# Moving weight combinations from VectorE to GpSimd in the first steps of a two-layer FFN kernel

## The chip, the cores and the metric

The kernel runs on one core of one Trainium2 chip. The metric is the device time of that core in microseconds (us), from one launch. Engines go by the profile's names: PE (TensorE), PEld (its weight loads), DVE (VectorE), ACT (ScalarE), POOL (GpSimd), SP (SyncE, which issues most of the loads). ACTq, SPq and POOLq are the engines' instruction queues.

## The reference

Only the first layer's feed-forward product matters here. With x of 32 x 128 x 2048, seen as 4096 rows of 2048:

```python
out = jnp.einsum('bsd,od->bso', x, W) + bias
xa  = jnp.einsum('bsd,erd->ebsr', x, A)
upd = jnp.einsum('ebsr,eor,e->bso', xa, Bf, coeffs * scales)
return out + upd
```

The x that enters it is first mixed by a kernel per batch row (eight mixed 128 x 128 matrices). Around the product there are a residual, a grouped convolution of nine taps, and a second feed-forward of 16 heads over permuted channels. All values are float32.

## The kernel before, in words

**One weight for both terms.** The low-rank update is folded into the weight: W' = W^T + A^T (w Bf), with w = coeffs * scales. W' is made in 16 blocks of 128 x 2048, `blocks`, named (kh, oh, kc): half of the contraction, half of the output, and one of four row tiles. `a_load` (L126) loads half h of A and then scales it by w on DVE (L135); `b_load` loads Bf. `w_load` (L154, on SP) loads a block of W^T. `w_make` (L160) makes one of the first four blocks by eight matmuls (L170), each pair added to the tile by DVE (L174), and stores the block with `w_store` (L158, a 1 MB DMA issued by POOL into `wb_d`). `w_make_two` (L203) makes two blocks at a time for the other twelve, in seven products (PE L208, DVE L211).

**Two levels of Strassen-Winograd.** The big product takes seven outer rounds, `ROUNDS` = P1, P2, P6, P7, P5, P3, P4, each over eight groups g of 512 rows of x: 56 steps. Step 0 is (P1, g = 0), step 8 is (P2, g = 0). Each step is one `multiply` (L318): seven inner products in the order P1, P2, P6, P5, P7, P3, P4, each over four row tiles kc, into the PSUM banks px, py, pz (PE L334). ACT copies a product to the result tile m_P where it is the first there (L329), DVE adds the others (L327). px goes on being accumulated in the later products, so PE waits until what stood there was read. `between(j)`, called after each inner product, hangs other work in: w loads for the next step (j = 2), row sums of W' (`row_sums`, L228, and L955/L956), all on DVE.

**Combinations.** An inner product needs sums of quarters. `x_combine` (L275) makes four for x on POOL (s_P, L285 to L288). For the weights a tile t has quarters b11, b12, b21, b22, and `inner_weights` (L230) makes t1 = b12 - b11, t2 = b22 - t1, b12 = b22 - b12 in place, t4 = b21 - t2: tiles P_t and the quarter b12 itself. Product P5 uses t1, P6 uses t2, P7 the new b12, P4 uses t4. In round P1 the first three are made on DVE (L873 to L875) piece by piece behind each `w_make`, and b12 on DVE in step 0 after `w_make_two` (L917), each behind an addition of the old b12 to the row sum (L916). `x_outer` (L298) makes two sums of three x tiles on POOL, in place, for later rounds (L302, L304), each stored by POOL (s_d, L262). `a_combine` makes sa (POOL), `b_combine` makes tb.

**What sets the order.** It is written out by hand: each engine runs its instructions in program order. All large tiles share 24 slots of 1 MB (`slot`), so a new tile waits for the last use of an older one, stores included. For step i the loop does, in order: x loads and `x_combine` of step i + 1, `x_outer`, `inner_weights` of the next round (only in rounds P2 and later, in the last step of the round), in round P1 `w_make_two` for two more blocks, `multiply`. In round P1 the combinations for P2 come behind the last `multiply` of the round.

Of the kernel before, what the change touches and what calls it, by code (L numbers as in the profile page):

```python
# [11 lines left out]
ALU = mybir.AluOpType  # L12
# [4 lines left out]
P = 128  # L17
B = 32
L = 2048
QW = 512  # L20
# [12 lines left out]
NG = B // GB  # L33
# [14 lines left out]
ROUNDS = ("P1", "P2", "P6", "P7", "P5", "P3", "P4")  # L48
# [3 lines left out]
def adaln_ffn_kernel(  # L52
# [16 lines left out]
    nc = tc.nc  # L69
# [8 lines left out]
    def slot(name, shape=(P, L)):  # L78
        return big.tile(list(shape), FP, name=name, tag="s")
# [46 lines left out]
    def a_load(h, k0, k1):  # L126
        for ki in range(2):
            i0 = (2 * h + ki) * QW
            nc.sync.dma_start(
                a_sb[h][:, :, ki, k0:k1].rearrange("p c k i -> p c (k i)"),  # L130
                A[:, :, i0 + k0 * P : i0 + k1 * P],
            )
        for c in range(2):
            cols = a_sb[h][:, c, :, k0:k1]
            nc.vector.tensor_scalar(cols, cols, wsc[:, c : c + 1], None, ALU.mult)  # L135

    def b_load(h, q, o0=0, n=QW):
        i0 = (2 * h + q) * QW + o0
        nc.sync.dma_start(bf_sb[h][:, :, q, o0 : o0 + n], BfT[:, :, i0 : i0 + n])
# [12 lines left out]
    def w_load(kh, oh, kc):  # L152
        t = slot(f"w_{kh}{oh}{kc}", (P, 2, 2, QW))
        nc.sync.dma_start(t.rearrange("p k o c -> p (k o c)"), WT[kh, oh, kc])  # L154
        return t
# [4 lines left out]
    def w_make(k, t):  # L160

        kh, oh, kc = k
        for oi in range(2):
            for ki in range(2):
                pw = bank()

                n = QW // 2 if k == (0, 0, 0) and oi == 0 else QW
                for o0 in range(0, QW, n):
                    for c in range(2):
                        nc.tensor.matmul(  # L170
                            pw[:, o0 : o0 + n], lhsT=a_sb[kh][:, c, ki, kc],
                            rhs=bf_sb[oh][:, c, oi, o0 : o0 + n], start=(c == 0), stop=(c == 1),
                        )
                nc.vector.tensor_tensor(t[:, ki, oi], pw, t[:, ki, oi], ALU.add)  # L174
                done(pw)
        w_store(k, t)
# [50 lines left out]
        for ki in range(2):  # L227
            nc.vector.tensor_tensor(wsum[:, oh], wsum[:, oh], t[:, ki], ALU.add)  # L228

    def inner_weights(name, ts):  # L230

        t1, t2, t4 = (slot(f"{name}_t{k}", (P, 4, QW)) for k in (1, 2, 4))
        tt = nc.gpsimd.tensor_tensor
        for kc, t in enumerate(ts):
            b11, b12, b21, b22 = (t[:, ki, oi] for ki in range(2) for oi in range(2))
            tt(t1[:, kc], b12, b11, ALU.subtract)
            tt(t2[:, kc], b22, t1[:, kc], ALU.subtract)  # L237
            tt(b12, b22, b12, ALU.subtract)
            tt(t4[:, kc], b21, t2[:, kc], ALU.subtract)
        return weights(ts, t1, t2, t4)  # L240

    def weights(ts, t1, t2, t4):
        return {
            "P1": [t[:, 0, 0] for t in ts], "P2": [t[:, 1, 0] for t in ts],
            "P3": [t[:, 1, 1] for t in ts], "P7": [t[:, 0, 1] for t in ts],
            "P4": [t4[:, kc] for kc in range(4)], "P5": [t1[:, kc] for kc in range(4)],
            "P6": [t2[:, kc] for kc in range(4)],
        }
# [596 lines left out]
    nc.sync.dma_start(cs, coeffs)  # L845
    nc.vector.tensor_tensor(wsc, cs[:, 0:2], cs[:, 2:4], ALU.mult)
    a_load(0, 0, 1)
    b_load(0, 0, 0, QW // 2)
    b_load(0, 0, QW // 2, QW // 2)
    b_load(0, 1)  # L850
    a_load(0, 1, 4)
    wt = {k: w_load(*k) for k in blocks[0:2]}
    xs = {0: [x_load(0, 0, 0)]}
    for k in blocks[2:4]:
# [7 lines left out]
    lhs, sa, tb = {}, {}, {}  # L862
    sa[0] = a_combine(0, nc.gpsimd.tensor_tensor)
    first = [wt.pop(k) for k in blocks[0:4]]
    t1, t2, t4 = (slot(f"P1_t{k}", (P, 4, QW)) for k in (1, 2, 4))
    for kc, t in enumerate(first):
        k = blocks[kc]
        w_make(k, t)
        made.append(k)
        if kc == 1:  # L870
            lhs[0] = x_combine(*steps[0], xs.pop(0))
        tt = nc.vector.tensor_tensor
        tt(t1[:, kc], t[:, 0, 1], t[:, 0, 0], ALU.subtract)  # L873
        tt(t2[:, kc], t[:, 1, 1], t1[:, kc], ALU.subtract)
        tt(t4[:, kc], t[:, 1, 0], t2[:, kc], ALU.subtract)  # L875
    rhs = weights(first, t1, t2, t4)
    tb[1] = b_combine(1, nc.vector.tensor_tensor)
    a_load(1, 0, 4)
    unsummed, unsummed_first = [], list(first)
# [9 lines left out]
    for i, (r, g) in enumerate(steps):  # L889
        ri = i // NG  # L890
        last_round = ri + 1 == len(ROUNDS)
        if i + 1 < len(steps):
            if i + 1 not in xs:
                xs[i + 1] = x_loads(*steps[i + 1])
            if not last_round:
                lhs[i + 1] = x_combine(*steps[i + 1], xs.pop(i + 1))
                x_outer()
        if i + 2 < len(steps) and ri > 0 and not last_round:
            xs[i + 2] = x_loads(*steps[i + 2])
        if i == 0:  # L900
            olds_load(0)
        if i + 1 < len(steps) and not last_round:
            olds_load(i + 1)
        if g == NG - 1 and 0 < ri < len(ROUNDS) - 1:
            nxt = inner_weights(ROUNDS[ri + 1], [nxt[kc] for kc in range(4)])

        if ri == 0:
            ks = blocks[4 + 2 * g : 6 + 2 * g]
            if ks:
                two = [wt.pop(k) for k in ks]  # L910
                w_make_two(ks, two, sa[ks[0][0]], tb[ks[0][1]])
                made.extend(ks)
                if g == 0:
                    for kc, t in enumerate(first):
                        b12 = t[:, 0, 1]
                        nc.vector.tensor_tensor(wsum[:, 0, 1], wsum[:, 0, 1], b12, ALU.add)  # L916
                        nc.vector.tensor_tensor(b12, t[:, 1, 1], b12, ALU.subtract)  # L917
                if g == 1:
                    sa[1] = a_combine(1, nc.gpsimd.tensor_tensor)
                if g == 3:  # L920
                    tb[0] = b_combine(0, nc.gpsimd.tensor_tensor)
                for k, t in zip(ks, two):
                    unsummed.append((k[1], t))
                    if k[:2] == (1, 0):
                        nxt[k[2]] = t
        elif ri + 1 < len(ROUNDS):
            for k, combine in waiting.items():
                nxt[k] = combine()
            waiting = {}
            if 2 <= g < 6:  # L930
                waiting[g - 2] = outer_weights(ROUNDS[ri + 1], g - 2)

        if last_round and g == 0:
            late_loads()
        if last_round and g == 2:

            late["te"] = mix.rearrange("p (k r) c -> p k r c", k=2)
            nc.sync.dma_start(mix.rearrange("p k c -> p (k c)"), te_d)
        k0 = 3 * (g - NG)
        if last_round:  # L940
            stage(k0, stage_first)

        def between(j):
            b = (ri - 1) * (NG - 2) + g
            if ri > 0 and g < NG - 2 and b < B and j < KEXP // 2:
                mixed_kernel(b, (2 * j, 2 * j + 1))
            if ri == 0 and j == 2:
                for k in blocks[6 + 2 * g : 8 + 2 * g]:
                    wt[k] = w_load(*k)
            if ri == 0 and j in (1, 3) and unsummed:  # L950
                row_sums(*unsummed.pop())
            if ri == 0 and j == 5 and unsummed_first:
                t = unsummed_first.pop(0)
                tt = nc.vector.tensor_tensor
                tt(wsum[:, 0, 0], wsum[:, 0, 0], t[:, 0, 0], ALU.add)  # L955
                tt(wsum[:, 0], wsum[:, 0], t[:, 1], ALU.add)  # L956
            if last_round:
                if j == 3 and i + 1 < len(steps):
                    lhs[i + 1] = x_combine(*steps[i + 1], xs.pop(i + 1))
                    olds_load(i + 1)  # L960
                if j in (2, 4):
                    stage(k0 + j // 2, stage_first)
                if j % 2:
                    stage_third(k0 + j // 2)
                else:
                    stage(k0 + j // 2, stage_second)

        multiply(r, g, lhs.pop(i), rhs, olds.pop(i), between)
        next(chain, None)
        if last_round and g >= 6:  # L970
            pair(g - 6)
        if last_round and g == 7:
            rings()
            gather_two(0)
        if g == NG - 1 and ri + 1 < len(ROUNDS):
            if ri == 0:
                nxt = inner_weights(ROUNDS[ri + 1], [nxt[kc] for kc in range(4)])
            rhs = nxt
            nxt = {}

# [83 lines left out]
```

## Time and profile before

| | us |
|---|---|
| median of three runs | 2672.01 (2669.6 to 2672.71) |
| profiled execution | 2672.8 |
| its span, first to last instruction | 2671.0 |
| PE busy | 2624.4 |
| DVE busy | 1404.4 |
| POOL busy | 1117.0 |
| ACT busy | 535.2 |

The span is what the profile pages and all times on its axis refer to; 1.8 us lie around it. A line of a timeline gives the start, the duration, the engine, the line of the kernel, what is written from what, how many instructions are merged, and in brackets how long the engine was idle before and what ended that. A line of waits reads: who waited for whom, total, times, longest. A line of windows gives the stretch, its length, the busy time of each engine with its instruction count, the clock granted to PE (1.00 is full), the mean share of the DMA engines and GB/s.

### The profile page before, as it was taken

To read this page: it belongs to the slowest core of one execution; us is meant where nothing else is said; L and a number is where in the kernel's file an instruction comes from. 1 tells how busy PE (TensorE), PEld (TensorE's weight loads), DVE (VectorE), ACT (ScalarE), POOL (GpSimd) and SP (SyncE) were. 2 spreads that over 40 slices of the span, in tenths; PEclk is the share of its full clock that TensorE was granted. 3 is DMA by queue.
4 is the path that set the end of the run, shared out by engine and by line. 5 is a ranking of instruction groups with operands and counts; after the bars stand their busy time and mean duration, and the time that the engine had idled before them with its cause. 6 is when DMAs were issued, how large, how long until landed. Compare 5 with 4: busy or idle time off the path is not lost.

```text
span 2671.0 us, 19893 instructions
## 1 busy us (share of the span) xinstructions
PE 2624.4 (98%) x6484; PEld 1233.8 (46%) x6484; DVE 1404.4 (53%) x2188; ACT 535.2 (20%) x1103; POOL 1117.0 (42%) x750
## 2 busy tenths in 40 slices
PE   7999999999999999999998999999999999999998
PEld 3444444444444444444444554544555544555543
DVE  5766145233344355454266666666666666666610
ACT  0100100000000000000001144444444444444432
POOL 4554455624736521755333333434333343333222
PEclk8999999999999999999999999999999999999999
DMA  8776548445456366555576788777787777877532
GB/s 330 298 298 265 210 182 327 184 154 209 188 228 256 145 267 267 218 211 232 201 250 183 253 298 272 225 231 234 242 253 225 229 227 233 250 235 235 164 127 87
DMA packets 183607, 609.16 MB, mean 228 GB/s; under 512 B 16848, under 2 KB 88016, under 8 KB 139088
## 3 DMA queue, kind: packets, MB, share of 16 engines
q1 hardware_dynamic: 148928, 466.40, 49.7%
q0 software_dynamic: 34144, 140.53, 15.3%
q10 hardware_dynamic: 432, 0.96, 0.1%
q8 instruction: 52, 0.85, 0.1%
q14 instruction: 51, 0.42, 0.0%
HBM read 364.03 MB, written 210.24 MB: 215 GB/s over the span
## 4 chain that ended last, share of the span: by engine, by line
PE 90%; DVE 5%; DMA 2%; POOL 1%; issue 1%; SPq 0%; ACT 0%; POOLq 0%; DVEq 0%
PE bank L334 46%; PE bank L679 16%; PE bank L690 16%; PE bank L537 6%; PE bank L447 4%; PE bank L208 2%; DVE ags L409 2%; DMA a_sb<-in_A 1%; DMA w<-in_WT 1%; DVE u L327 0%; DMA xt<-in_xT 0%; DVE vb L519 0%; DVE wsum L916 0%; DMA ws<-in_ffw 0%; DVE vb L516 0%
## 5 line engine op out<-in xcount | busy, mean ns | idle before, releaser
L679 PE MATMUL bank<-t,ws 128*128 128x512 f32 x1024 | 460.4, 592 | 0.4 <-DMA ws<-in_ffw 0.4
L690 PE MATMUL bank<-gl,ws 128*128 128x512 f32 x1024 | 460.2, 592 | 0.0
L682 ACT ACTIVATE gl<-bank 128x512 f32<-128x512 f32 x512 | 306.1, 598 | 446.4 <-PE bank L679 444.1
L334 PE MATMUL bank<-P_t,s_P 128*128 128x512 f32 x896 | 393.9, 592 | 1.5 <-POOL P_t L237 1.5
L327 DVE TENSOR_TENSOR u<-bank,u 128x512 f32<-128x512 f32 x280 | 187.3, 687 | 387.4 <-PE bank L334 378.3
L697 POOL DMA_INDIRECT out<-t,orow x128 | 152.8, 1194 | 567.5 <-DVE t L695 501.2
L690 PEld LDWEIGHTS bank<-gl,ws 128*128 128x128 f32 x1024 | 194.9, 190 | 232.7 <-issue 230.3
L679 PEld LDWEIGHTS bank<-t,ws 128*128 128x128 f32 x1024 | 194.7, 190 | 227.0 <-issue 219.1
L334 PE MATMUL bank<-wo_P,s_P 128*128 128x512 f32 x640 | 285.4, 596 | 5.5 <-DVE u L327 5.5
L334 PEld LDWEIGHTS bank<-P_t,s_P 128*128 128x128 f32 x896 | 170.4, 190 | 215.0 <-issue 211.9
L438 ACT ACTIVATE bank<-w,aggb 128x512 f32<-128x512 f32 x128 | 80.8, 684 | 894.5 <-DMA w<-w_d 876.4
L695 DVE TENSOR_TENSOR t<-bank,t 128x512 f32<-128x512 f32 x128 | 87.9, 687 | 315.5 <-PE bank L690 315.5
L430 POOL TENSOR_TENSOR x<-x,fb 128x1024 f32<-128x1024 f32 x64 | 155.3, 2446 | 220.8 <-DMA x<-in_x 192.0
L327 DVE TENSOR_TENSOR p<-bank,p 128x512 f32<-128x512 f32 x112 | 77.4, 691 | 246.7 <-PE bank L334 244.9
L334 PEld LDWEIGHTS bank<-wo_P,s_P 128*128 128x128 f32 x640 | 121.6, 191 | 161.3 <-issue 148.5
L409 DVE SCALAR_TENSOR_TENSOR ags<-mix,att_bc,ags 128x128 f32<-128x128 f32 x224 | 182.9, 816 | 4.5
L334 PE MATMUL bank<-wo_P,xt 128*128 128x512 f32 x384 | 169.0, 592 | 0.0
L663 POOL DMA_INDIRECT t<-hx_d,row x128 | 125.0, 977 | 56.4 <-issue 25.5
L285 POOL TENSOR_TENSOR s_P<-xt 128x512 f32<-128x512 f32 x40 | 52.0, 1300 | 227.3 <-DMA xt<-in_xT 200.7
L334 PE MATMUL bank<-P_t,xt 128*128 128x512 f32 x320 | 144.1, 593 | 2.6 <-DVE m_P L327 1.6
L537 PE MATMUL bank<-va,tw_l 128*128 128x256 f32 x512 | 122.4, 380 | 8.9 <-DVE va L520 7.6
L537 PEld LDWEIGHTS bank<-va,tw_l 128*128 128x128 f32 x512 | 96.8, 190 | 51.3 <-issue 36.4
(159 smaller groups left out, 2864.5 us busy)
## 6 DMA issues: line engine op xcount, KB each, us to landing
xt<-in_xT SPq DMA_DIRECT2D x64, 1024.0 KB, 8.8
u<-u_d SPq DMA_DIRECT2D x40, 1024.0 KB, 10.6
wo_P<-wb_d SPq DMA_DIRECT2D x36, 1024.0 KB, 12.5
u<-c_d SPq DMA_DIRECT2D x64, 512.0 KB, 6.0
x<-in_x SPq DMA_DIRECT2D x32, 1024.0 KB, 7.8
xg<-x SPq DMA_DIRECT2D x256, 128.0 KB, 5.9
hx_d<-x1t SPq DMA_DIRECT2D x32, 1024.0 KB, 5.4
hx_d<-ht SPq DMA_DIRECT2D x32, 1024.0 KB, 7.2
```

The source lines that it names most:

```text
L327: nc.vector.tensor_tensor(to, ps, to, ALU.add)
L334: nc.tensor.matmul(ps, lhsT=lhs[k][:, bass.ts(kc, P)], rhs=rhs[k][kc], start=first and kc == 0, stop=last and kc == 3, skip_group_check=True,)
L409: nc.vector.scalar_tensor_tensor(ag, mix[:, k], att, ag, ALU.mult, ALU.add)
L430: nc.gpsimd.tensor_tensor(xt[:, f : f + 2], xt[:, f : f + 2], late["fb"][:, f : f + 2], ALU.add)
L447: nc.tensor.matmul(pm, lhsT=ag, rhs=u[:, f], start=False, stop=True, skip_group_check=True)
L537: nc.tensor.matmul(out, lhsT=w[:, 2 * i + r], rhs=rhs, start=first and r == 0, stop=last and r == 1, skip_group_check=True,)
L663: nc.gpsimd.indirect_dma_start(out=t.rearrange("p k t -> p (k t)"), out_offset=None, in_=hx_d[g].rearrange("l k t -> l (k t)"), in_offset= ...
L679: nc.tensor.matmul(pu, lhsT=w[:, m * P : (m + 1) * P], rhs=t[:, 0], start=True, stop=True)
L682: nc.scalar.activation(gl[m], pu, AF.Gelu)
L690: nc.tensor.matmul(pd, lhsT=w[:, (MC + m) * P : (MC + m + 1) * P], rhs=gl[m], start=(m == 0), stop=(m == MC - 1),)
L695: nc.vector.tensor_tensor(t[:, 1], pd, t[:, 1], ALU.add)
L697: nc.gpsimd.indirect_dma_start(out=out, out_offset=bass.IndirectOffsetOnAxis(ap=orow[:, g, h : h + 1], axis=0), in_=t[:, 1], in_offset=None,)
```

## The change

The scale is split from `a_load` as `a_scale`; for the second half of A it is called in step 1, behind `w_make_two`, instead of ahead of step 0. `inner_weights` gets a hook, `between`, and round P1 uses it too: all four combinations of the first four blocks, and the addition of the old b12 to the row sum, are now on POOL, each block's right behind its `w_make`; `x_combine` of step 0 stands ahead of the third block's. The combinations for round P2 are issued in the step before the last of round P1, ahead of its `w_make_two` place and `multiply`, instead of behind the last `multiply`.

```diff
-        for c in range(2):
+    def a_scale(h, k0, k1):
+        for c in range(2):
             cols = a_sb[h][:, c, :, k0:k1]
             nc.vector.tensor_scalar(cols, cols, wsc[:, c : c + 1], None, ALU.mult)
...
-    def inner_weights(name, ts):
+    def inner_weights(name, ts, between=lambda kc: None):
...
         for kc, t in enumerate(ts):
+            between(kc)
...
-    t1, t2, t4 = (slot(f"P1_t{k}", (P, 4, QW)) for k in (1, 2, 4))
-    for kc, t in enumerate(first):
-        k = blocks[kc]
-        w_make(k, t)
-        made.append(k)
-        if kc == 1:
+
+    def make_first(kc):
+        t = first[kc]
+        w_make(blocks[kc], t)
+        made.append(blocks[kc])
+        if kc == 2:
             lhs[0] = x_combine(*steps[0], xs.pop(0))
-        tt = nc.vector.tensor_tensor
-        tt(t1[:, kc], t[:, 0, 1], t[:, 0, 0], ALU.subtract)
-        tt(t2[:, kc], t[:, 1, 1], t1[:, kc], ALU.subtract)
-        tt(t4[:, kc], t[:, 1, 0], t2[:, kc], ALU.subtract)
-    rhs = weights(first, t1, t2, t4)
+        nc.gpsimd.tensor_tensor(wsum[:, 0, 1], wsum[:, 0, 1], t[:, 0, 1], ALU.add)
+
+    rhs = inner_weights("P1", first, make_first)
...
-        if g == NG - 1 and 0 < ri < len(ROUNDS) - 1:
+        if g == NG - (1 if ri else 2) and ri < len(ROUNDS) - 1:
             nxt = inner_weights(ROUNDS[ri + 1], [nxt[kc] for kc in range(4)])
...
-                if g == 0:
-                    for kc, t in enumerate(first):
-                        b12 = t[:, 0, 1]
-                        nc.vector.tensor_tensor(wsum[:, 0, 1], wsum[:, 0, 1], b12, ALU.add)
-                        nc.vector.tensor_tensor(b12, t[:, 1, 1], b12, ALU.subtract)
                 if g == 1:
+                    a_scale(1, 0, 4)
                     sa[1] = a_combine(1, nc.gpsimd.tensor_tensor)
...
-            if ri == 0:
-                nxt = inner_weights(ROUNDS[ri + 1], [nxt[kc] for kc in range(4)])
```

More of the change, by code (lines that the diff above doesn't have):

```diff
@@ L239, in inner_weights @@
             tt(t4[:, kc], b21, t2[:, kc], ALU.subtract)
-        return weights(ts, t1, t2, t4)
-    def weights(ts, t1, t2, t4):
         return {
@@ L847, in adaln_ffn_kernel @@
     a_load(0, 0, 1)
+    a_scale(0, 0, 1)
     b_load(0, 0, 0, QW // 2)
@@ L851, in adaln_ffn_kernel @@
     a_load(0, 1, 4)
+    a_scale(0, 1, 4)
     wt = {k: w_load(*k) for k in blocks[0:2]}
```

## The prediction

> **What bounds the kernel now.** I read the page first: TensorE (PE) is busy nearly all the span, so only its gaps can be won.
>
> ```profile
> PE 2624.4 (98%) x6484; PEld 1233.8 (46%) x6484; DVE 1404.4 (53%) x2188; ACT 535.2 (20%) x1103; POOL 1117.0 (42%) x750
> ```
>
> Next, what PE waited for in the first 350 us, where all edits lie (total, times, longest):
>
> ```profile
> PE bank L208 <- DVE w L211: 13.6, 3, 12.8
> PE bank L334 <- DVE w L917: 1.7, 3, 1.3
> PE bank L334 <- DVE m_P L327: 1.6, 1, 1.6
> PE bank L334 <- POOL P_t L237: 1.5, 1, 1.5
> ```
>
> These are the edits' targets: 12.8 us once, 3.3 us in step 0's multiply, 1.5 us at the change of round. Then the windows of those stretches (busy PE, PEld, DVE, ACT, POOL; granted clock; DMA share):
>
> ```profile
> 36.00:52.00 16.00, 3.17 (x9) 1.18 (x7) 7.11 (x12) 0.00 (x0) 0.54 (x1) 0.74 1.02 420
> 52.00:64.00 12.00, 12.00 (x22) 5.23 (x23) 8.30 (x13) 0.00 (x0) 11.31 (x7) 0.78 0.40 165
> 64.00:92.00 28.00, 24.73 (x56) 10.13 (x55) 26.24 (x18) 3.18 (x5) 15.20 (x9) 1.00 0.75 287
> ```
>
> PE stands still to 51.9 and restarts at a reduced clock: 20 matmul records take 11.4 us there, 8.6 at the later pace (56 in 24.03). DMA is saturated to 52. Timeline of DVE:
>
> ```profile
> 49.75 1.42 DVE L135 TENSOR_SCALAR a_sb<-a_sb,wsc 128x1024 f32<-128x1024 f32 x2 [8.79 <-DMA a_sb<-in_A]
> 51.09 2.48 DVE L211 TENSOR_TENSOR w<-bank,w 128x512 f32<-128x512 f32 x4
> 67.82 5.36 DVE L917 TENSOR_TENSOR w<-w 128x512 f32<-128x512 f32 x1
> 73.10 5.47 DVE L916 TENSOR_TENSOR wsum<-wsum,w 128x512 f32<-128x512 f32 x1
> ```
>
> The evictions stood behind a scale that waited for its load. Timelines of POOL and ACT, and the load queue's waits:
>
> ```profile
> 52.29 1.26 POOL L285 TENSOR_TENSOR s_P<-xt 128x512 f32<-128x512 f32 x1 [15.07 <-DMA xt<-in_xT]
> 57.30 4.53 POOL L302 TENSOR_TENSOR xt<-xt,xt 128x2048 f32<-128x2048 f32 x1
> 62.13 0.56 POOL L262 DMA_DIRECT2D s_d<-xt  x1 [0.30 <-POOL xt L302]
> 62.71 4.52 POOL L304 TENSOR_TENSOR xt<-xt,xt 128x2048 f32<-128x2048 f32 x1
> ```
> ```profile
> 66.96 1.28 ACT L329 ACT_TABLE_LOAD   x1 [66.96 <-PE bank L334]
> 68.25 0.58 ACT L329 COPY m_P<-bank 128x512 f32<-128x512 f32 x1
> ```
> ```profile
> SPq L154 <- DMA s_d<-xt: 51.7, 3, 32.1
> ```
>
> This is the hidden second chain. The first s_d store lands at 62.1 + 4.5 = 66.6, and ACT's semaphore instructions for L329 run at 66.6: m_P of step 0 reuses the slot of an x tile that L302/L304 and this store must release. PE's first product ends at about 66.9, so now the tie costs nothing. The w loads of step 1 wait for the next two s_d stores (issued 71.7 and 79.3, landing in 5.0 and 10.8 us). A late POOL can thus stop PE twice; the instruction order of the changed kernel, with the semaphore each instruction waits on, keeps all three ties. Last, landings of the wb_d stores (minimum/median/maximum, first 110 us):
>
> ```profile
> DMA to landing us min/median/max: 8.4/9.2/11.9
> ```
>
> **The Trainium skill.** "DMA: Bandwidth & Descriptors", section "Anatomy of one DMA — SWDGE (gpsimd) path", prices a GpSimd DMA at 2.0 us plus bytes at 436 GB/s: estimate 4.4 us for 1 MB. The trace agrees on free engines (4.1 and 4.5 for the first s_d stores), not under the load stream: 8.4, 8.7, 9.4, 9.1 for the first four wb_d. "SBUF — State Buffer", section "SBUF: two separate sides", says a DVE operation with two SBUF inputs and a GpSimd one lock each other out; agreed, 5.4 us against 0.69 above. "TensorE: Matmul & The Clock Gate", section "What's actually happening", gives half clock after an idle window of about 3.4 us; the 0.74 and 0.78 agree.
>
> **The change, part by part.**
>
> *Scale a step later.* Two DVE instructions (1.42 us) move behind step 1's evictions (w_make_two); the load's place on SP is unchanged. sa[1], after them on POOL, is first needed in step 2: at nothing; that step's work covers 1.4 us. The last L174 ends at 36.4, the four b_combine take 2.6, so L211 runs at 39.0 and PE resumes at 39.8, not 51.9. Both w tiles land by 39.6. At full clock (10 pairs of 0.86) step 0's multiply starts at **48.4**, not 63.3.
>
> *DVE to POOL.* DVE loses 12 combinations and 8 sum/b12 instructions. PE sets the pace of w_make (DVE already waits for it at its end), so this gains nothing before 36. POOL gains 20 of 1.26 us (16 P_t rows of the round change run 321.06 to 341.23). New is a wait: b12 overwrites what the wb_d store of its tile reads, and in the changed order it waits for that store's landing. Behind it on POOL stand t4, the next piece's store and combinations, and x_combine of steps 0 and 1, then x_outer (L302/L304) with its stores:
> - sa ends 18.7 (last one 1.3, unstretched). Store 0 then, landing 18.7 + 8.4 = 27.0; b12, t4 to 29.6.
> - Store 1 lands 29.6 + 9.4 = 39.0; to 41.6.
> - Store 2 lands 41.6 + 9.1 = 50.7, behind x_combine (5.0) and three combinations: no wait; to 53.5.
> - Store 3: 53.5 + 4.5 = 58.0, as on free engines (the last x load landed at 57.1 with four stores ahead of it; with three, a megabyte or 2.4 us sooner); to 60.55.
> - Step 1's x_combine ends 60.55 + 5.0 = 65.6, when L302 starts: **8.3 us later** than 57.3.
>
> These combinations themselves are in time: the last t2 is made at 57.8, PE could use it at 57.9. But the first s_d store lands at 65.6 + 9.3 = 74.9; table load 1.28, copy 0.58: PE's third product, which adds to the bank that ACT must first copy, starts at about **76.9**; without the tie it would be 55.3. It has idled 21 us, so half clock: before lost 2.8 in such a restart; bounds 1.7 to 3.4 (half of one to two windows of 3.4), I take 2.55. Five products of 3.43 are 17.2: multiply ends 76.9 + 17.2 + 2.55 = **96.6**, against 91.7. So the 12.8 us and the 3.3 us are both spent: **+4.9**. Row sums stuck behind L302/L304 now fall beside products with slack; that cover gone costs up to 1.5.
>
> Step 1's second w load, landing at 90.0 before, lands at 98.3; PE reaches its need at about 100.2: slack 2. Bounds 0 and +3. Behind that load on SP stand the p_d store and step 2's x loads, which need multiply's end anyway. The late wb_d stores (6, 12, 17 us) are read only rounds later: at nothing.
>
> *P2's combinations one step sooner.* 16 POOL instructions (20.2 us) pass x_combine of step 8, and on SP nothing is reordered. On the clock of before they run from 304.4, where the last x_outer store is issued, to 324.6 (now 341.2); x_combine of step 8 ends at 329.6 (now 321.1), its second row at 327.1, PE's use of it is at 334.6. The 1.5 us wait goes: **-1.5** (bounds 0, -2).
>
> Between 104 and 325 PE idles 1 us in 221, and loads follow PE, so nothing absorbs the shift. The sum is +4.9 - 1.5 = **+3.4**. The profiled execution took 2672.8 (span 2671.0), 0.8 above the median: 2676.2 there, **2675.5** on the median's scale. About 0.2% (5.3 us) is what a measurement of this kernel can tell from no change.
>
> **The rivals.**
> 1. *Slower: the stores land later still.* Price: each us on the chain of stores 0, 1 and 3 is a us of PE. Later wb_d stores took 11.9 at worst; 11 us for the first two and 6.5 for store 3 add 2.6 + 1.6 + 2 = 6.2: +9.6. It decides from +1.9 on. For it: the loads saturate DMA (share 1.02). Against it: the first four lie within 8.4 to 9.4. The step 1 load landing over 2 us late ends there too.
> 2. *Faster: the chain is short.* If stores landed in 4.5 us, the x load (52.2) would again start step 1's x_combine: L302 at 57.3, third product at 68.6, multiply ends 88.3, so -3.4 - 1.5 = -4.9; with that load 2.4 us earlier (1 MB less store traffic before it), -7.3. Against it: those stores run beside saturated loads.
> 3. *Slot tie not binding.* If m_P did not wait, multiply would end at 72.4, but the w load at 98.3 would hold the second block: about +5.9 - 1.5 = +4.4. Same answer by another wait.
>
> **How the numbers follow.** Late chain as sized, with its bounds (+0.5 to +7): 0.68, of which about a quarter lies over +5.3. Rival 3: 0.10, half over. Rival 1: 0.12. Rival 2: 0.10, of which 0.07 beyond -5.3. So faster 0.07, same 0.59, slower 0.34. Range 2670.5 to 2681.5: -1.5 to +9.5, leaving out the rest of rival 2 and the worst of rival 1.
>
> **What would show it.** Right: PE runs w_make_two without a gap over 2 us by 40; b12 (L241 of the changed kernel) on POOL waiting for wb_d twice, 4 and 5 us; L302 first at about 65.6; PE's gap moved into step 0's multiply, some 20 us, released by ACT L329; no P_t wait near 340. Wrong: L302 before 60, no gap after 55, or a second gap, in step 1's w_make_two.

## The result, and the profile after

The changed kernel takes 2676.2 us (median of 22 runs, 2672.47 to 2679.8), the kernel before 2672.8 (22 runs, 2669.6 to 2675.89): ratio 1.0013, 95% interval 1.0006 to 1.0019, or +3.5 us (+1.6 to +5.1). The forecast was +3.4. The profiled execution took 2674.35, span 2672.6.

```profile
PE 2623.7 (98%) x6484; PEld 1234.4 (46%) x6484; DVE 1385.7 (52%) x2168; ACT 535.1 (20%) x1103; POOL 1142.4 (43%) x770
```

DVE is 19 us less busy and POOL 25 us more, as 20 instructions moved; PE's own work is the same. Lines have moved: w_make_two is L210 with its evictions L213, b12 is L241, the row sums are L230. What PE waited for in the first 350 us, from the table of waits after:

```profile
PE bank L334 <- ACT m_P L329: 22.3, 1, 22.3
PE bank L210 <- DVE w L213: 1.3, 3, 0.6
```

The four waits that the edits aimed at are gone, but for rests of at most 0.6 us, and one new one of 22.3 us stands in their place. PE's timeline shows where:

```profile
39.92 5.39 PE L210 MATMUL bank<-tb,sa 128*128 128x512 f32 x12 [0.57 <-DVE w L213]
48.58 7.03 PE L334 MATMUL bank<-w,xt 128*128 128x512 f32 x16
77.87 8.96 PE L334 MATMUL bank<-P_t,s_P 128*128 128x512 f32 x16 [22.26 <-ACT m_P L329]
96.96 3.60 PE L210 MATMUL bank<-bf_sb,a_sb 128*128 128x512 f32 x8
```

Sixteen matmuls in a line are two products. PE starts step 0's multiply at 48.58 instead of 63.29, does two products, and stands before the third. Step 1's w_make_two starts at 96.96 instead of 91.66: the 14.7 us won are lost, and 5.3 more. POOL's and ACT's timelines give the chain behind that wait:

```profile
27.69 1.27 POOL L241 TENSOR_TENSOR w<-w 128x512 f32<-128x512 f32 x1 [4.11 <-DMA wb_d<-w]
39.60 1.27 POOL L241 TENSOR_TENSOR w<-w 128x512 f32<-128x512 f32 x1 [5.03 <-DMA wb_d<-w]
52.59 1.26 POOL L241 TENSOR_TENSOR w<-w 128x512 f32<-128x512 f32 x1 [1.07 <-DMA wb_d<-w]
66.84 4.49 POOL L302 TENSOR_TENSOR xt<-xt,xt 128x2048 f32<-128x2048 f32 x1
71.62 0.57 POOL L262 DMA_DIRECT2D s_d<-xt  x1 [0.30 <-POOL xt L302]
```
```profile
75.94 1.28 ACT L329 ACT_TABLE_LOAD   x1 [75.94 <-DMA s_d<-xt]
```

b12 waits for the landing of the block's own store, three times, 10.2 us in all. So x_outer starts at 66.84 instead of 57.30, its first store lands at 75.9, and only then may ACT write m_P. At the change of round the third and fourth products of step 8 now run as one piece:

```profile
339.95 7.03 PE L334 MATMUL bank<-P_t,s_P 128*128 128x512 f32 x16
```

Before, the third was split by 1.5 us of waiting. The fifth starts at 346.82 instead of 343.26: +3.6. The two profiled spans differ by 1.6 only; after 350 us PE's waits sum to 12.6 us in this execution and 15.9 in the one of before, in stages that the change doesn't touch, and the medians, which differ by 3.4, do not carry that difference.

### The profile page after: what moved, and what is told of

The parts are those of the page before. It is cut to its first block, busy times and chain, and to the rows that moved or that the text cites. A ratio compares the mean times of both kernels' runs of the same rounds, so it can differ in the third digit from the quotient of the medians.

```text
span 2672.6 us, 19881 instructions
## 1 busy us (share of the span) xinstructions
PE 2623.7 (98%) x6484; PEld 1234.4 (46%) x6484; DVE 1385.7 (52%) x2168; ACT 535.1 (20%) x1103; POOL 1142.4 (43%) x770
## 4 chain that ended last, share of the span: by engine, by line
PE 92%; DVE 4%; POOL 2%; issue 1%; DMA 1%; SPq 0%; ACT 0%; POOLq 0%; DVEq 0%; ACTq 0%
PE bank L334 47%; PE bank L679 16%; PE bank L690 16%; PE bank L537 6%; PE bank L447 4%; PE bank L210 2%; DVE ags L409 2%; DVE u L327 0%; DVE vb L516 0%; DMA ws<-in_ffw 0%; DVE vb L519 0%; DVE va L517 0%; DMA a_sb<-in_A 0%; DVE va L518 0%; POOL wsum L874 0%
## 5 line engine op out<-in xcount | busy, mean ns | idle before, releaser
L334 PE MATMUL bank<-P_t,s_P 128*128 128x512 f32 x896 | 395.6, 595 | 22.3 <-ACT m_P L329 22.3
L663 POOL DMA_INDIRECT t<-hx_d,row x128 | 125.4, 980 | 54.6 <-issue 25.2
## 6 DMA issues: line engine op xcount, KB each, us to landing
wo_P<-wb_d SPq DMA_DIRECT2D x36, 1024.0 KB, 12.6
```

What stands on the lines that cost most here:

```text
L334: nc.tensor.matmul(ps, lhsT=lhs[k][:, bass.ts(kc, P)], rhs=rhs[k][kc], start=first and kc == 0, stop=last and kc == 3, skip_group_check=True,)
L663: nc.gpsimd.indirect_dma_start(out=t.rearrange("p k t -> p (k t)"), out_offset=None, in_=hx_d[g].rearrange("l k t -> l (k t)"), in_offset= ...
```

## The experiments

Two theories went in. **Chain**: a gain of PE before its third product of step 0 is worth nothing, since that product waits for POOL's x_outer, its store and ACT; POOL's lateness is the price, and the waits on landing stores make it. **Additive**: each edit is worth what the wait it removes shows.

All ratios are to the kernel before, run beside each kernel (medians 2673.5 and 2673.7 us).

**1. The later scale alone** (scale_only).

```diff
-        for c in range(2):
+    def a_scale(h, k0, k1):
+        for c in range(2):
...
                 if g == 1:
+                    a_scale(1, 0, 4)
```

> The kernel before with only the scale of A's second half moved to step 1. Chain theory (in step 0 PE can go no further than product P2 until GpSimd has finished the first x_outer sum, its store has landed and ACT has copied the first product): PE starts step 0's multiply at 48.4 instead of 63.3, then stands until about 68.6, restarts at half clock, and step 1's w_make_two starts at about 88.0 instead of 91.7: -3.7 us. Additive theory (each edit is worth what the wait it removes shows): 12.1 us of stall and 2.8 us of half clock go, -14.9 us.

Ratio 0.9990 (0.9982 to 0.9999): -2.7 us, between -4.8 and -0.3. POOL's and PE's timelines:

```profile
54.30 1.73 POOL L287 TENSOR_TENSOR s_P<-xt 128x512 f32<-128x512 f32 x1 [17.41 <-DMA xt<-in_xT]
60.55 4.49 POOL L304 TENSOR_TENSOR xt<-xt,xt 128x2048 f32<-128x2048 f32 x1
```
```profile
50.03 7.03 PE L336 MATMUL bank<-w,xt 128*128 128x512 f32 x16
71.58 10.10 PE L336 MATMUL bank<-P_t,s_P 128*128 128x512 f32 x16 [14.52 <-ACT m_P L331]
```

Removing a wait of 12.8 us bought a wait of 14.5 us. That excludes the additive -14.9. The expected 68.6 came at 71.58: the x load landed at 54.2 instead of 52.2 in this execution, and x_combine took 6.3 us instead of 5.0 beside DVE operations with two inputs from SBUF. In the trace step 1's w_make_two starts at 91.82, 0.2 later than before, so the -2.7 of the times is not seen in this stretch; it lies at the edge of what is resolved, and its cause is not shown. One candidate lies in later stages, behind two short gaps of PE near 1405 and 1465 us that both traces have: eight matmuls there take 3.60 and 3.67 us in this trace and 5.29 and 5.30 in the one of before, at a granted clock of 0.5 for some 3 us each time. That is 3.4 us. The mean granted clock of the runs points the same way (0.9952 in 13 runs, 0.9944 in 35 of before).

**2. P2's combinations alone** (p2_only): only the condition on g, and no call behind the round.

```diff
-        if g == NG - 1 and 0 < ri < len(ROUNDS) - 1:
+        if g == NG - (1 if ri else 2) and ri < len(ROUNDS) - 1:
```

> The kernel before with only the combinations for round P2 issued one step sooner. Both theories: the 1.5 us wait of PE at 337.4 goes and nothing else moves: -1.5 us, step 1's w_make_two stays at 91.7, step 8's third product follows its second without a gap.

Ratio 0.9989 (0.9981 to 0.9997): -2.9 us, between -5.1 and -0.8, which holds the -1.5. PE's timeline has the two products in one piece:

```profile
334.38 7.03 PE L334 MATMUL bank<-P_t,s_P 128*128 128x512 f32 x16
```

**3. The move to POOL alone** (pool_only): the changed kernel with the scale called right behind `a_load(1, 0, 4)` again, and P2's combinations back behind the last multiply.

> The kernel before with only the first blocks' combinations on GpSimd piece by piece; the scale stays ahead of step 0 and the combinations for P2 behind round P1. Chain theory: PE's early stall on the scale comes back (w_make_two resumes at about 47.7 as the loads end sooner) but lies wholly in front of the wait on ACT's copy, so L302 starts at 66.8 and step 1's w_make_two at 97.0 all the same: +5.3 us. Additive theory: the whole change without its gains of 14.9 and 1.5 us, about +20 us.

Ratio 1.0019 (1.0011 to 1.0028): +5.1 us, between +2.9 and +7.5. PE's timeline:

```profile
49.53 7.52 PE L210 MATMUL bank<-tb,sa 128*128 128x512 f32 x12 [10.67 <-DVE w L213]
77.77 8.78 PE L334 MATMUL bank<-P_t,s_P 128*128 128x512 f32 x16 [10.43 <-ACT m_P L329]
```

The early stall is back, and the third product starts at 77.77, within 0.1 us of the whole change. So beside the move the later scale is worth nothing: 10.67 us of stall and 10.43 of the second wait share what was 22.3. That PE resumed at 49.53 and not at 47.7 is a miss that cost nothing: the scale took 3.1 us instead of 1.4 beside POOL's operations.

**4. The same operations without the waits on stores** (b12_late): the four b12 behind the fourth block's t4.

```diff
-            tt(b12, b22, b12, ALU.subtract)
+            if name != "P1":
+                tt(b12, b22, b12, ALU.subtract)
             tt(t4[:, kc], b21, t2[:, kc], ALU.subtract)
+        if name == "P1":
+            for t in ts:
+                tt(t[:, 0, 1], t[:, 1, 1], t[:, 0, 1], ALU.subtract)
```

> The changed kernel with the four b12 = b22 - b12 of the first blocks put behind the fourth block's t4, so that GpSimd does the same 20 operations but no longer waits for each store before the next block. Chain theory, with the waits on the stores' landing as its cause: the fourth block is done at 46.6, the four b12 at about 51.7, step 1's x_combine waits for its x load (about 52.2), L302 starts at about 57.3 and step 1's w_make_two at about 88: -3.7 - 1.5 = -5.2 us against the kernel before. Rival, the 20 operations themselves make GpSimd late: L302 stays at about 66 and the time at about +3.4 us.

Ratio 0.9981 (0.9970 to 0.9991): -5.1 us, between -8.0 and -2.4; against the changed kernel some 8 or 9 us less. POOL's and PE's timelines:

```profile
49.65 4.95 POOL L246 TENSOR_TENSOR w<-w 128x512 f32<-128x512 f32 x4
59.57 4.49 POOL L306 TENSOR_TENSOR xt<-xt,xt 128x2048 f32<-128x2048 f32 x1
```
```profile
70.61 10.07 PE L338 MATMUL bank<-P_t,s_P 128*128 128x512 f32 x16 [10.98 <-ACT m_P L333]
```

The same 20 operations, and x_outer starts 7.3 us sooner than in the changed kernel. That is the 10.2 us of waits less 0.9 (the first store was issued that much later here) less some 1.7 by which four POOL operations were longer beside DVE's b_combine; 0.3 is left over. It was expected at 57.3; those 2.3 us are the miss. The rival, that the operations themselves make POOL late, falls: they leave x_outer 2.3 us behind the kernel before, where the changed kernel is 9.5 behind. But the -5.1, so close to the -5.2 expected, is partly luck: step 1's w_make_two starts at 90.81, not at 88, and at step 8 the trace is 2.6 us ahead of the one of before.

**5. Five us more on POOL's chain** (pool_plus5): in the changed kernel, step 1's x_combine twice.

```diff
+        for _ in range(2 if (r, g) == ("P1", 1) else 1):
```

> The changed kernel with step 1's x_combine done twice on GpSimd (the second time the same values), 5.0 us more of GpSimd work behind the four blocks and before L302. Chain theory: so far PE's third product of step 0 started 11.03 us after the first x_outer instruction in each kernel where it waited for ACT; it then starts 5.0 us later, at 82.9, and the whole time grows by the same 5.0: about +8.4 us against the kernel before. Rival, GpSimd is a side path with slack and the loss has another source (DMA traffic, a clock drop later): no change against the changed kernel, +3.4.

Ratio 1.0039 (1.0025 to 1.0052): +10.4 us, between +6.7 and +13.9. POOL's and PE's timelines:

```profile
72.37 4.49 POOL L303 TENSOR_TENSOR xt<-xt,xt 128x2048 f32<-128x2048 f32 x1
```
```profile
83.40 9.48 PE L335 MATMUL bank<-P_t,s_P 128*128 128x512 f32 x16 [27.93 <-ACT m_P L330]
```

x_outer 5.53 us later, the third product 5.53 us later. In five kernels PE's third product comes a fixed time after the first x_outer instruction: 66.84 to 77.87 (changed), 66.73 to 77.77 (pool_only), 60.55 to 71.58, 59.57 to 70.61, 72.37 to 83.40: 11.03 or 11.04 us each. In the three kernels of the experiments below the time is longer, 11.48, 13.82 and 14.90 us, where x_outer itself or its store took longer (4.94 us for 4.49; landings of 6.9 and 8.0 us for 4.2). From ACT's release by that store to the third product it is 1.93 or 1.94 us in all eight. That POOL is on the path with slope one is shown.

**6. The change without the move** (scale_p2): the edits of 1 and 2 together.

> The kernel before with the later scale and P2's combinations one step sooner, without the move to GpSimd. Chain theory, with the 91.8 that the later scale alone gave at step 1's w_make_two: 0.1 - 1.5 = about -1.5 us by the trace. Additive theory: -14.9 - 1.5 = -16 us.

Ratio 0.9986 (0.9979 to 0.9993): -3.7 us, between -5.6 and -1.9. PE's timeline:

```profile
71.02 9.77 PE L336 MATMUL bank<-P_t,s_P 128*128 128x512 f32 x16 [11.35 <-ACT m_P L331]
```

The additive -16 is out; the expected -1.5 was too small by about 2 us. In its trace step 1's w_make_two starts at 90.92, 0.9 before the run of experiment 1, and at step 8 it is 1.5 us ahead of the kernel before, as expected; the other 2 us are not explained. The move to POOL is the one part of the change that costs, and even with its waits cured (experiment 4) it is not measurably better than leaving it out.

**7 and 8. The tie loosened** (outer0_first, outers_first): the four late b12, and step 0's x_outer ahead of them and of step 1's x_combine; in the second kernel step 1's x_outer too.

```diff
+                if i == 0:
+                    x_outer()
+                    for t in first:
+                        nc.gpsimd.tensor_tensor(t[:, 0, 1], t[:, 1, 1], t[:, 0, 1], ALU.subtract)
+                    outer.append((1, xs[1]))
+                    x_outer()
                 lhs[i + 1] = x_combine(*steps[i + 1], xs.pop(i + 1))
```

The two lines of `outer.append` and the second `x_outer` are only in outers_first, where x_combine no longer appends step 1's tiles.

> The kernel with the four late b12, and step 0's x_outer put ahead of them and of step 1's x_combine. Chain theory: L302 starts at about 49.7, so PE's third product at 60.7, about 1 us after its second, at full clock; step 0's multiply ends at 77.9. Then the second tie shows: step 1's second w load waits for the store of step 1's first x_outer sum and lands at about 91, PE stands about 9 us inside step 1's w_make_two, which ends at about 101.4 instead of 103.7: with P2's gain -3.8 us in all. Rival, only the first tie counts and the load is covered: w_make_two ends at 89.9, -15 us.

Ratio 0.9986 (0.9980 to 0.9993): -3.7 us, between -5.3 and -1.9. PE's timeline:

```profile
61.92 7.13 PE L335 MATMUL bank<-P_t,s_P 128*128 128x512 f32 x16 [0.83 <-ACT m_P L330]
90.21 7.14 PE L210 MATMUL bank<-tb,sa 128*128 128x512 f32 x10 [4.74 <-DVE w L213]
```

DVE's timeline, and the load queue's waits, name the second tie:

```profile
89.46 2.48 DVE L213 TENSOR_TENSOR w<-bank,w 128x512 f32<-128x512 f32 x4 [5.18 <-DMA w<-in_WT]
```
```profile
SPq L156 <- DMA s_d<-xt: 58.4, 3, 22.7
```

Of the first tie 0.8 us is left. The second shows at once, inside step 1's w_make_two, where PE stands 1.6 and 4.7 us (9 were expected) and restarts at half clock. It takes back most of what was won: step 1's w_make_two starts 11.6 us sooner than in b12_late (79.19 for 90.81), its multiply only 2.2 sooner, at 100.62; 101.4 was expected.

> The same, with step 1's x_outer also ahead of step 1's x_combine. Chain theory: the store that step 1's second w load waits for is issued at about 70 and lands at 74.6, the load lands at about 81, before PE needs it at 82.2: step 1's w_make_two ends at about 89.9 instead of 103.7, -13.8 - 1.5 = about -15 us. Rival, a later tie (step 2's loads wait for stores that x_combine now delays) gives it back: between -4 and -10 us, with a new gap of PE after 110.

Ratio 0.9977 (0.9968 to 0.9986): -6.1 us, between -8.6 and -3.7, the fastest version by its median (2666.58 us); it beats both kernels, by less than half of what was expected; its lead over b12_late is not resolved. ACT's and PE's timelines:

```profile
62.74 1.28 ACT L330 ACT_TABLE_LOAD   x1 [62.74 <-DMA s_d<-xt]
```
```profile
64.68 8.71 PE L335 MATMUL bank<-P_t,s_P 128*128 128x512 f32 x16 [3.56 <-ACT m_P L330]
97.14 7.03 PE L335 MATMUL bank<-w,xt 128*128 128x512 f32 x16
```

Step 1's multiply starts at 97.14 instead of 103.67; 89.9 was expected. The second tie is gone. Three things make nearly all of the 7.2 us that are missing. The first x_outer store, issued at 54.6 while the loads still ran, took 8.0 us to land instead of 4.2, so the third product came at 64.68 and not at 60.7: 4.0 us. It started at half clock: 1.7. And a row sum that took long beside POOL's x_outer and x_combine stopped PE before its last product: 1.3.

PE had begun the multiply at 54.09 only, after a wait of 4.4 us on DVE's evictions. The w loads were not its cause, as the second had landed at 41.0. DVE came to the evictions at 42.9, since b_combine took 6.5 us beside POOL's combinations and not 2.6:

```profile
41.24 1.74 DVE L199 TENSOR_TENSOR tb<-bf_sb,tb 128x512 f32<-128x512 f32 x1
42.91 2.47 DVE L213 TENSOR_TENSOR w<-bank,w 128x512 f32<-128x512 f32 x4
```

In the changed kernel POOL was waiting for a store just then, and b_combine took its 2.6 us. The rival's number came true (-4 to -10), its cause did not: the gap of PE after 110 us is 1.2 us, and DVE's row sums end it, not a load.

**The traces beside the times.** How far each trace is ahead of the one of before (-) or behind it (+) when the fifth product of step 8 starts, and the difference of the times:

| kernel | step 8 in the trace, us | times, us |
|---|---|---|
| the whole change | +3.6 | +3.5 |
| scale_only | 0.0 | -2.7 |
| p2_only | -2.0 | -2.9 |
| pool_only | +5.6 | +5.1 |
| b12_late | -2.6 | -5.1 |
| pool_plus5 | +10.2 | +10.4 |
| scale_p2 | -1.5 | -3.7 |
| outer0_first | -2.5 | -3.7 |
| outers_first | -6.9 | -6.1 |

Each trace is one execution. Its number lies inside the interval of the times but for scale_only and scale_p2, where 2 to 3 us of the times do not show by step 8.

## Why the prediction was right, point by point

- **Scale later:** PE was to resume w_make_two at 39.8 and start multiply at 48.4; 39.92 and 48.58. Right, and worth nothing beside the move (experiment 3).
- **Waits on the stores:** two waits of 4 and 5 us were named; 4.11 and 5.03, and a third of 1.07, where none was forecast, since store 2 took 10.5 us, not 9.1. Stores 0, 1 and 3 took 8.6, 9.4 and 4.2. x_outer was to start at 65.6, it started at 66.84; the third wait is most of that 1.2.
- **The tie of m_P's slot:** the third product was to start at 76.9, it did at 77.87. The step from ACT's release to the product holds in eight kernels to 0.01 us, so it is shown. Rival 3 (tie not binding) is out.
- **Half clock at the restart:** 2.55 was taken between 1.7 and 3.4. The third and fourth products together ran 8.96 us instead of 7.03: 1.9. The granted clock was 0.50 from 77.9 to about 81. This error and that of the store cancel in part, so multiply's end came at 96.96 for 96.6. The closeness of the sum is partly luck.
- **Row sums beside slack:** four of them took 12.7 us on DVE behind x_outer, and no wait of PE names them. Right.
- **Step 1's second w load:** it landed some 2 us later than the 98.3 predicted; DVE waited for it, PE did not:

```profile
100.42 4.32 DVE L213 TENSOR_TENSOR w<-bank,w 128x512 f32<-128x512 f32 x7 [1.71 <-DMA w<-in_WT]
```

  Here the slack was nearly used up; in pool_only the same load cost PE 0.4 us.
- **P2's combinations sooner:** -1.5, borne out by the trace of the changed kernel and of experiment 2.
- **Rival 1** (stores still later) came true for one store by 1.4 us, below the 1.9 from which it decides. **Rival 2** (a short chain) did not happen; experiment 4 shows it in part where the waits are taken out: x_outer at 59.57 for the 57.3 of this rival, the end of multiply at 90.81 for 88.3. The time of -5.1 agrees with its price of -4.9 better than these steps do.

## What to carry to other kernels

When a stall goes, look for the next thing that the freed engine needs and when that is ready: here PE was ready for its third product at 55.6 us, and a buffer slot three engines away let it start at 77.9. Before an in-place operation moves closer to a store of the same tile, price the landing of that store on busy DMA engines, and everything queued behind the waiting engine. Two waits that cover each other cannot be added: undo one part alone before crediting it.

## What the runs showed of the hardware that was not expected

- A 1 MB store from POOL landed in 4.1 to 4.5 us on free DMA engines and, under the load stream of the first 60 us, in 8.0 us (outers_first) to 10.7 (pool_plus5). By the Trainium skill's "DMA: Bandwidth & Descriptors", section "Anatomy of one DMA — SWDGE (gpsimd) path", the estimate is 4.4 us, so the stores beside the loads took 1.8 to 2.4 times as long. outers_first lost 3.8 us to it at the very store that it had moved forward.
- The half-clock restart cost 1.7 us (outers_first) to 3.1 us (scale_only) on two products of 7.03, so a gap of PE has a price of its own. The length of the gap does not give it: 3.6 us of standing cost 1.7, 14.5 cost 3.1, 27.9 cost 2.5. A gap of 2.62 us in scale_only was followed by a granted clock of 1.00, one of 2.63 in scale_p2, at the same place of the program, by 0.50 for some 3 us.
- GpSimd's 128x512 operations took 1.6 to 1.75 us instead of 1.26 beside DVE operations of the same size with two SBUF inputs, and those took 1.6 to 1.75 instead of 0.69. So an engine that stops waiting can slow its neighbour: b_combine took 6.5 us instead of 2.6 in outers_first.
